# The middle of each FP4 quantisation on GpSimd instead of VectorE

## The chip, the cores and the metric

The kernel runs on one core of one Trainium2 chip. The metric is device time in microseconds (us), the median of several runs; smaller is better. Engines are named as the profile names them: PE is TensorE (matmuls and transposes), PEld its weight loads, ACT is ScalarE, DVE is VectorE, POOL is GpSimd, and SP is the queue that issues all DMAs here.

## What is computed

The input `x` has 8 batches of 1024 tokens with 512 features, in float32. One block is computed from the layer-normalised tokens, with two branches that are added to `x`:

```python
xn = _layernorm(x)
x = x + attn(xn, W_attn, b_attn, W_proj, b_proj) + ffn(xn, w_gate, w_up, w_down)
```

`attn` is causal attention with 16 heads of 32 features. `ffn` is a gated network with 1408 hidden features, in which the inputs and the weights of each of its three products are first quantised to FP4 and back:

```python
def fp4_quant_dequant(x):               # blocks of 16 along the last dimension
    scale = max(abs(block)) / 6.0       # one per block, at least 1e-12
    xn = block / scale
    idx = searchsorted(_MID, abs(xn))   # to the nearest of 0 .5 1 1.5 2 3 4 6
    return _GRID[idx] * sign(xn) * scale
def fp4_linear(x, w):
    return einsum(fp4_quant_dequant(x), fp4_quant_dequant(w))
h = silu(fp4_linear(x, w_gate)) * fp4_linear(x, w_up)
return fp4_linear(h, w_down)
```

The change is about the engine that does parts of `fp4_quant_dequant`.

## The kernel before

**Tiles.** Tokens go in tiles of 128 (64 in all), two tiles making a "twin" of 256 tokens. `prepare` (L387) normalises a twin, transposes it on PE (`transposed`, L324), and computes queries, keys and values (`project`, L435), which go to DRAM and come back by units of two heads (64 units). `scored` (L547) computes a unit's scores (L603), their row minima on DVE (L616, L619) and the exponentials on ACT (L575, into `part`). `weigh` (L666) transposes these on PE (L708), copies the result from PSUM on ACT (L711, into `pr`; a memset on POOL at L716 clears the corner), and multiplies with the values (L686). `network` (L749) does the FFN of a twin in six jobs of 512 columns (the sixth of 256): the products with `wgT` and `wuT` (L803), silu on ACT (L815) and the product with it on DVE (L820), giving `hid`; then `down` multiplies the quantised `hid` with `wdT` (L765). `finish` (L880) projects the attention's result (L895, L896, L904, L909) and stores the sum. All of it shares five PSUM banks (`Banks`, L180).

**Quantisation.** An instance of `Quantised` (L258) is a piece of at most 128x512 that is quantised in place. There are three kinds: 34 pieces of the weights (`weights_quantised`, L334; 28 of them while the first 16 tiles are prepared, six later), two halves of `xqT` for each of the 32 twins (`quantised`, L415), and the six `hid` of a twin (`hidden`, L819). Its steps, all on DVE before the change: for `xqT` and `hid` a transpose in 32x32 blocks (L263); the maximum of each block of 16 (L300); three small operations on the scales (L303 to L305); the product with the inverse scale (L317); the exponent of every element by a bit mask (L309) and a limit and factor on it (L312), which together give `step`; `step` added and subtracted (L319, L320), which rounds; the product with the scale (L321); and the transpose back.

**The order of the work** is written out when the kernel is built, by a plan with a clock in it: each engine has a time `free[...]`, each instruction adds a cost that the code states, and `merge` (L983) takes steps from several streams (attention's two halves, the network, the preparation, `finish`) so that PE has work whose inputs the plan believes ready. Every engine then executes its own queue in that written order, waiting on semaphores. The steps of pieces to be quantised lie in the list `background`; `passed` (L161) issues the next step of the first piece whenever the plan's DVE is about to be idle:

```python
idle = max(clock[0], free["dve"] - FILL, background[0].after)
```

A stream that needs a piece waits until the plan's `ready()` (L275), an estimate from the costs still left on DVE. The plan is not told how two engines affect one another.

**What POOL does before the change:** a power for each tile's normalisation (L378, 128x1), the memset at L716, and the bias added to a tile of the residual (L781, 128x512).

## Time and profile before

| | |
|---|---|
| median of 3 runs | 4223.45 us (4218.54 to 4223.89) |
| the profiled execution | 4220.1 us |
| its span, first to last instruction | 4218.2 us |
| mean granted PE clock | 0.994 of full speed |
| busy in the span | PE 4064.8, DVE 3061.9, ACT 2170.3, POOL 145.1 us |
| read from and written to HBM | 399.51 and 168.30 MB, 135 GB/s over the span |

The profile is one execution. A line of it names an engine, a line of the kernel (L321), an operation, and the tile written and those read (`hid<-hid,scale`). "PE bank L328 <- DVE hid L321" means that PE's instruction of line 328 waited, with PE idle, for DVE's instruction of line 321. A PE that is busy is not necessarily at its peak, since the ends of matmuls are modelled. The span falls into three parts: up to about 400 us the weights are quantised and the first tiles prepared; then attention, network and preparation run together, in a pattern that repeats every 127.3 us (a twin) until about 3200 us, when all tiles are prepared, and without preparation until about 4100 us; in the rest the last twin's network and the last eight tiles are finished.

### The profile page before, as it was taken

The numbers are of one execution on the slowest core, as the hardware profiler recorded it, in microseconds if no ns is written. First come the engines' busy times: TensorE is split into PE (matmuls) and PEld (weight loads), VectorE is DVE, ScalarE is ACT, GpSimd is POOL, SyncE is SP. The second block draws the span as 40 slices with busy tenths as digits, with TensorE's granted clock in tenths as the row PEclk, the third lists the DMA queues.
The fourth block names the chain that finished last, engine by engine and source line by source line (L and its number), as shares of the span: only waits on it lengthen the run. The fifth ranks groups of instructions, "written<-read, shape, count | busy, mean of one in ns | idle before, by whom it ended". The sixth has DMA issues, their size and how long they took to land.

```text
span 4218.2 us, 66169 instructions
## 1 busy us (share of the span) xinstructions
PE 4064.8 (96%) x22868; PEld 3008.8 (71%) x22868; DVE 3061.9 (73%) x7128; ACT 2170.3 (51%) x5342; POOL 145.1 (3%) x202
## 2 busy tenths in 40 slices
PE   8889999999999999999999999999999999999997
PEld 7766777777777777777777777777777666666665
DVE  7886776776766687766777766777666777777775
ACT  2245555555555555555555555555555555555540
POOL 0000000000000000000000000000000000000000
PEclk9999999999999999999999999999999999999999
DMA  6654443455555555555555555555554433333314
GB/s 194 197 162 120 123 118 113 130 143 148 160 143 152 147 142 153 165 140 146 155 143 149 160 142 150 150 143 152 157 144 116 116 91 95 95 94 96 96 57 129
DMA packets 550894, 572.21 MB, mean 136 GB/s; under 512 B 112416, under 2 KB 415520, under 8 KB 550560
## 3 DMA queue, kind: packets, MB, share of 16 engines
q1 hardware_dynamic: 550560, 567.99, 48.3%
q8 instruction: 181, 2.97, 0.3%
q14 instruction: 153, 1.25, 0.1%
HBM read 399.51 MB, written 168.30 MB: 135 GB/s over the span
## 4 chain that ended last, share of the span: by engine, by line
PE 87%; ACT 4%; DVE 3%; DMA 1%; issue 1%; SPq 0%; ACTq 0%; DVEq 0%
PE bank L803 29%; PE acc L765 14%; PE bank L708 11%; PE bank L448 9%; PE bank L603 8%; PE y L686 7%; PE bank L904 5%; PE bank L493 4%; ACT pr L711 2%; ACT part L575 1%; DVE bank L619 1%; PE bank L328 0%; DMA qs<-inv_kept 0%; DMA out_dram<-qs 0%; ACT full L504 0%
## 5 line engine op out<-in xcount | busy, mean ns | idle before, releaser
L711 ACT COPY pr<-bank 128x512 f32<-128x512 f32 (+1 forms) x1280 | 665.3, 548 | 811.2 <-PE bank L708 761.1
L575 ACT ACTIVATE part<-bank,neg 128x512 f32<-128x512 f32 (+3 forms) x1536 | 881.3, 583 | 183.5 <-DVE neg L619 151.3
L603 PE MATMUL bank<-ks,qs 128*128 128x512 f32 (+3 forms) x1536 | 715.8, 486 | 28.0 <-ACT pr L711 14.6
L708 PE MATMUL bank<-ident,part 128*128 128x128 f32 x4608 | 672.4, 274 | 32.2 <-ACT pr L711 17.2
L803 PE MATMUL bank<-xqT,wgT 128*128 128x256 f32 x2816 | 674.5, 384 | 19.4 <-ACT pr L711 17.4
L803 PE MATMUL bank<-xqT,wuT 128*128 128x256 f32 x2816 | 667.8, 381 | 0.0
L708 PEld LDWEIGHTS bank<-ident,part 128*128 128x128 f32 x4608 | 548.4, 141 | 160.5 <-ACT part L575 34.3
L765 PE MATMUL acc<-wdT,hid 128*128 128x512 f32 x1408 | 655.0, 595 | 3.1 <-DVE hid L263 3.1
L803 PEld LDWEIGHTS bank<-xqT,wgT 128*128 128x128 f32 x2816 | 516.5, 190 | 120.9 <-ACT pr L711 26.7
L803 PEld LDWEIGHTS bank<-xqT,wuT 128*128 128x128 f32 x2816 | 515.8, 190 | 68.1 <-issue 7.4
L616 DVE TENSOR_REDUCE neg<-bank 128x1 f32<-128x512 f32 x512 | 350.5, 685 | 292.1 <-PE bank L603 287.6
L603 PEld LDWEIGHTS bank<-ks,qs 128*128 128x128 f32 x1536 | 281.2, 189 | 248.1 <-issue 144.2
L619 DVE CUSTOM_DVE_ANT_0 bank<-bank,mask,neg 128x128 f32<-128x128 f32 (+3 forms) x512 | 284.5, 556 | 155.0 <-PE bank L603 123.6
L765 PEld LDWEIGHTS acc<-wdT,hid 128*128 128x128 f32 x1408 | 247.9, 190 | 208.2 <-issue 200.7
L686 PE MATMUL y<-pr,vs 128*32 128x256 f32 (+1 forms) x5120 | 356.0, 371 | 0.0
L448 PE MATMUL bank<-xnT,wa 128*128 128x256 f32 x1536 | 351.6, 382 | 0.2 <-ACT part L575 0.2
L448 PEld LDWEIGHTS bank<-xnT,wa 128*128 128x128 f32 x1536 | 287.4, 191 | 47.7 <-issue 10.8
L575 ACT ACTIVATION_READ_ACCUMULATOR part<-bank,neg 128x1 f32 x1536 | 314.2, 205 | 0.0
L619 DVE CUSTOM_DVE_ANT_0 bank<-bank,mask 128x128 f32<-128x128 f32 (+3 forms) x512 | 251.8, 496 | 84.4 <-PE bank L603 56.2
L460 ACT ACTIVATE full<-bank,bqk 128x256 f32<-128x256 f32 x256 | 107.3, 470 | 396.6 <-PE bank L448 335.5
L820 DVE TENSOR_TENSOR hid<-hid,bank 128x512 f32<-128x512 f32 x192 | 123.3, 642 | 253.4 <-PE bank L803 252.5
L263 DVE STREAM_TRANSPOSE hid<-hid 128x512 f32<-128x512 f32 (+1 forms) x384 | 245.9, 653 | 5.4
(79 smaller groups left out, 4115.9 us busy)
## 6 DMA issues: line engine op xcount, KB each, us to landing
wa<-in_L_attn_W_attn_dram SPq DMA_DIRECT2D x146, 512.0 KB, 3.7
qs<-qk_kept SPq DMA_DIRECT2D x512, 128.0 KB, 4.2
ks<-qk_kept SPq DMA_DIRECT2D x512, 128.0 KB, 4.1
wp<-in_L_attn_W_proj_dram SPq DMA_DIRECT2D x81, 512.0 KB, 3.8
qk_kept<-high SPq DMA_DIRECT2D x128, 256.0 KB, 3.0
qk_kept<-full SPq DMA_DIRECT2D x128, 256.0 KB, 3.0
y_kept<-yu SPq DMA_DIRECT2D x256, 128.0 KB, 2.4
yT<-y_kept SPq DMA_DIRECT2D x112, 256.0 KB, 3.5
```

What stands on the lines that cost most here:

```text
L263: turn = [(0.69, 0.0, lambda: nc.vector.transpose(out=xs, in_=xs))] if turned else []
L448: nc.tensor.matmul(pq[:, j, :], lhsT=halves[j][:, c, :], rhs=xnT[:, c, :], start=(c == 0), stop=(c == NC - 1),)
L575: nc.scalar.activation(parts[part][:, j * n : (j + 1) * n], banks.tiles[bank][:, j * n : (j + 1) * n], AF.Exp, bias=least, scale=1.0 if h ...
L603: nc.tensor.matmul(sc[:, j * n : (j + 1) * n], lhsT=un.qs[Q][:, r, i * P : (i + 1) * P], rhs=un.ks[h][:, r, :n], start=True, stop=True,)
L616: nc.vector.tensor_reduce(neg[:, 1, k : k + 1], one, AX.X, ALU.max, negate=True)
L619: nc.vector.tensor_tensor_reduce(one, one, mask[:, W - n :], scale=-1.0, scalar=neg[:, 1, k : k + 1] if Q else 3e38, op0=ALU.add, op1=ALU.min,
L686: nc.tensor.matmul(y[row : row + HD, base + q0 : base + QW], lhsT=un.vs[h][:, jj, r * HD : (r + 1) * HD], rhs=pr[:, r, q0:], start=(j < 2) ...
L708: nc.tensor.transpose(turned[:, r, i * P : (i + 1) * P], parts[part][:, at : at + P], ident)
L711: nc.scalar.copy(pr[:, :, i0 * P :], turned[:, :, i0 * P :])
L765: nc.tensor.matmul(twin.accs[i], lhsT=hqT[:, j, i * P : (i + 1) * P], rhs=wdT[:, n, :], start=(n == 0), stop=(n == NI - 1),)
L803: nc.tensor.matmul(job.g[:, j * QW : (j + 1) * QW], lhsT=wT[:, c, n * P : (n + 1) * P], rhs=job.twin.xqT[:, c, :], start=(c == 0), stop=(c ...
L904: nc.tensor.matmul(po, lhsT=yT[:, c, :], rhs=wp[:, c, :], start=(c == 0), stop=(c == NC - 1))
```

## The change

A piece can be `helped`: then the product with the inverse scale, the limit and factor (L312 before), the addition, the subtraction and the product with the scale are issued on POOL; the maximum, the scales, the exponents and the transposes stay on DVE. Pieces of `xqT` and `hid` are always helped; a piece of the weights is when the plan's POOL, with what is queued on it and 8.0 us more, would be through before the plan's DVE with 4.85 us more. In the order that results, 11 of the 34 weight pieces are. `passed` now takes the piece whose next step can start first, over both engines, and each step waits in the plan for the end of the piece's step before it and 0.2 us (`HOP`). `ready()` counts the load of both. The buffers of the scales grow from four to six, and `step` has one buffer for each engine in place of two.

```diff
--- before.py
+++ after.py
@@ -82,6 +82,8 @@
     LATE = 0.6
     SURE = 0.4
     FILL = 0.4
+    HELPED = 8.0
+    ALONE = 4.85
     HOP = 0.2
     TABLE = 1.3
     AHEAD_OF_OTHERS = 0.6
@@ -95,6 +97,7 @@
     p2 = ctx.enter_context(tc.tile_pool(name="p2", bufs=2))
     p3 = ctx.enter_context(tc.tile_pool(name="p3", bufs=3))
     p4 = ctx.enter_context(tc.tile_pool(name="p4", bufs=4))
+    p6 = ctx.enter_context(tc.tile_pool(name="p6", bufs=6))
     p8 = ctx.enter_context(tc.tile_pool(name="p8", bufs=8))
     dram = ctx.enter_context(tc.tile_pool(name="dram", bufs=6, space=DRAM))
     ps_g = ctx.enter_context(tc.tile_pool(name="ps_g", bufs=1, space=PSUM))
@@ -158,14 +161,20 @@
 
     background = []
 
+    def next_in_background():
+
+        first = {}
+        for one in background:
+            first.setdefault(one.left[0][0], one)
+        times = ((max(clock[0], free[e] - FILL, one.end - FILL, one.after - HOP), one) for e, one in first.items())
+        return min(times, key=lambda entry: entry[0], default=(float("inf"), None))
+
     def passed(us):
         end = clock[0] + us
         while True:
             first = min(waiting_list, key=lambda e: e.due, default=None)
             due = first.due if first is not None else float("inf")
-            idle = float("inf")
-            if background:
-                idle = max(clock[0], free["dve"] - FILL, background[0].after)
+            idle, one = next_in_background()
             if min(due, idle) > end:
                 break
             if due <= idle:
@@ -174,7 +183,7 @@
                 first.now()
             else:
                 clock[0] = idle
-                background[0].one()
+                one.one()
         clock[0] = end
 
     class Banks:
@@ -258,17 +267,23 @@
     class Quantised:
 
 
-        def __init__(self, src, w, xs, after=0.0, turned=False):
+        def __init__(self, src, w, xs, after=0.0, turned=False, helped=None):
             self.out, self.after, self.end = xs, after, 0.0
-            turn = [(0.69, 0.0, lambda: nc.vector.transpose(out=xs, in_=xs))] if turned else []
-            steps = turn + self.operations(src, w, xs) + turn
-            self.left = [(us + wide * w / CW, action) for wide, us, action in steps]
+            if helped is None:
+                helped = self.queue("pool") + HELPED < self.queue("dve") + ALONE
+            turn = [("dve", 0.69, 0.0, lambda: nc.vector.transpose(out=xs, in_=xs))] if turned else []
+            steps = turn + self.operations(src, w, xs, helped) + turn
+            self.left = [(engine, us + wide * w / CW, action) for engine, wide, us, action in steps]
             background.append(self)
 
+        def queue(self, engine):
+            behind = sum(us for one in background for e, us, _ in one.left if e == engine)
+            return max(clock[0], free[engine]) + behind
+
         def one(self):
-            us, action = self.left.pop(0)
+            engine, us, action = self.left.pop(0)
             action()
-            self.end = dve(us, self.after - HOP)
+            self.end = on(engine, us, max(self.end, self.after - HOP))
             if not self.left:
                 background.remove(self)
 
@@ -276,7 +291,9 @@
             if not self.left:
                 return self.end
             ahead = background[: background.index(self) + 1]
-            return max(clock[0], self.after) + 1.3 * sum(us for one in ahead for us, _ in one.left)
+            load = {e: sum(us for one in ahead for f, us, _ in one.left if f == e) for e in ("dve", "pool")}
+            own = sum(us for _, us, _ in self.left)
+            return max(clock[0], self.after) + max(own, 1.3 * load["dve"], load["pool"])
 
         def wait(self):
 
@@ -288,15 +305,16 @@
                 self.one()
             return self.out
 
-        def operations(self, src, w, xs):
+        def operations(self, src, w, xs, helped):
             nb = w // BLOCK
             blocks = lambda a: a.rearrange("p (n e) -> p n e", e=BLOCK)
             spread = lambda a: a.unsqueeze(2).broadcast_to([P, nb, BLOCK])
             scale, inv, step = [], [], []
+            name, eng, two, one = ("pool", nc.gpsimd, 1.28, 0.75) if helped else ("dve", nc.vector, 0.7, 0.43)
 
             def maximum():
-                scale.append(p4.tile([P, CW // BLOCK], F32, name="scale")[:, :nb])
-                inv.append(p4.tile([P, CW // BLOCK], F32, name="inv")[:, :nb])
+                scale.append(p6.tile([P, CW // BLOCK], F32, name="scale")[:, :nb])
+                inv.append(p6.tile([P, CW // BLOCK], F32, name="inv")[:, :nb])
                 nc.vector.tensor_reduce(scale[0], blocks(src), AX.X, ALU.max, apply_absolute_value=True)
 
             def scales():
@@ -304,21 +322,22 @@
                 nc.vector.reciprocal(inv[0], scale[0])
                 nc.vector.tensor_scalar_mul(inv[0], inv[0], 1.0 - 2.0**-24)
 
+            def exponents():
+                step.append(p2.tile([P, CW], F32, name=f"step_{name}", bufs=1)[:, :w])
+                nc.vector.tensor_scalar(step[0].bitcast(I32), xs.bitcast(I32), 0x7F800000, None, ALU.bitwise_and)
+
             def powers():
-                step.append(p2.tile([P, CW], F32, name="step")[:, :w])
-                nc.vector.tensor_scalar(
-                    step[0].bitcast(I32), xs.bitcast(I32), 0x7F800000, None, ALU.bitwise_and
-                )
-                nc.vector.tensor_scalar(step[0], step[0], 1.0, 1.5 * 2.0**22, ALU.max, ALU.mult)
+                eng.tensor_scalar(step[0], step[0], 1.0, 1.5 * 2.0**22, ALU.max, ALU.mult)
 
             return [
-                (0.68, 0.0, maximum),
-                (0.2, 0.5, scales),
-                (0.7, 0.0, lambda: nc.vector.tensor_tensor(blocks(xs), blocks(src), spread(inv[0]), ALU.mult)),
-                (0.87, 0.0, powers),
-                (0.7, 0.0, lambda: nc.vector.tensor_tensor(xs, xs, step[0], ALU.add)),
-                (0.7, 0.0, lambda: nc.vector.tensor_tensor(xs, xs, step[0], ALU.subtract)),
-                (0.7, 0.0, lambda: nc.vector.tensor_tensor(blocks(xs), blocks(xs), spread(scale[0]), ALU.mult)),
+                ("dve", 0.68, 0.0, maximum),
+                ("dve", 0.2, 0.5, scales),
+                (name, two, 0.0, lambda: eng.tensor_tensor(blocks(xs), blocks(src), spread(inv[0]), ALU.mult)),
+                ("dve", 0.43, 0.0, exponents),
+                (name, one, 0.0, powers),
+                (name, two, 0.0, lambda: eng.tensor_tensor(xs, xs, step[0], ALU.add)),
+                (name, two, 0.0, lambda: eng.tensor_tensor(xs, xs, step[0], ALU.subtract)),
+                (name, two, 0.0, lambda: eng.tensor_tensor(blocks(xs), blocks(xs), spread(scale[0]), ALU.mult)),
             ]
 
     def transposed(dst, src, n):
@@ -421,7 +440,7 @@
         nc.sync.dma_start(out=xqT, in_=twin.xnT)
         yield 0.0, clock[0] + 5.0, 0, 0.1
         halves = [xqT[:, c : c + NC // 2, :].rearrange("p c t -> p (c t)") for c in (0, NC // 2)]
-        working = [Quantised(half, NC // 2 * QW, half, clock[0], turned=True) for half in halves]
+        working = [Quantised(half, NC // 2 * QW, half, clock[0], turned=True, helped=True) for half in halves]
         for one in working:
             yield from one.wait()
             one.done()
@@ -820,7 +839,7 @@
             nc.vector.tensor_tensor(job.hid, job.hid, job.g, ALU.mult)
             end = dve(0.7, max(job.gated, clock[0] + 1.72))
             banks.back(job.bank, end)
-            job.hq = Quantised(job.hid, job.w, job.hid, end, turned=True)
+            job.hq = Quantised(job.hid, job.w, job.hid, end, turned=True, helped=True)
 
         def jobs():
             for twin in twins:
```

## The prediction

> **What bounds the kernel now.** I read the page first: busy shares, then the chain of waits. Columns of the first line: busy us (share of the span) x instructions.
>
> ```profile
> PE 4064.8 (96%) x22868; PEld 3008.8 (71%) x22868; DVE 3061.9 (73%) x7128; ACT 2170.3 (51%) x5342; POOL 145.1 (3%) x202
> ...
> PE 87%; ACT 4%; DVE 3%; DMA 1%; issue 1%; SPq 0%; ACTq 0%; DVEq 0%
> ```
>
> TensorE (PE) is the bound: 87% of the chain that ended last is PE. VectorE (DVE), which the change relieves, holds 3% of it. So no sum of DVE time saved is a gain; only PE's idle time is on offer. The table by stage says where that lies (stage, length, busy us of PE, PEld, DVE, ACT, POOL, granted PE clock, DMA):
>
> ```profile
> 0.00:400.00 400.00, 339.16 (x1774) 270.93 (x1774) 307.87 (x705) 156.93 (x385) 17.12 (x36) 0.94 0.59 172
> 400.00:4100.00 3700.00, 3632.11 (x20739) 2669.61 (x20738) 2688.94 (x6302) 2010.51 (x4953) 125.02 (x164) 1.00 0.48 132
> 4100.00:4218.00 118.00, 93.57 (x360) 68.23 (x358) 65.05 (x122) 2.88 (x6) 2.94 (x2) 0.99 0.41 118
> ```
>
> PE is idle 61 us in the first 400, 68 in the next 3700, 24 in the last 118. The waits of PE, first for the stage 0 to 400, then 400 to 4100 (us in total, times, longest):
>
> ```profile
> PE bank L328 <- DVE hid L321: 22.3, 9, 4.7
> PE bank L328 <- DVE xt L382: 15.6, 1, 15.6
> ```
> ```profile
> PE bank L803 <- ACT pr L711: 17.4, 38, 0.8
> PE bank L708 <- ACT pr L711: 15.3, 30, 0.8
> PE bank L603 <- ACT pr L711: 13.6, 35, 0.5
> PE bank L708 <- ACT part L575: 7.4, 28, 0.6
> ```
>
> At the start PE waits 22.3 us for quantised weights from DVE (the 15.6 are the first normalisation, which the change leaves alone). In the middle it waits for ScalarE (ACT) to empty PSUM banks, less than 1 us at a time; DVE stands behind only a part of that.
>
> **What the change takes off DVE.** The order of instructions shows which pieces move: all 64 halves of `xqT`, all 192 of the network's `hid` (160 of 512 columns, 32 of 256), and 11 of the 34 weight pieces; 23 stay on DVE. Per full piece DVE loses four two-input operations (rows of L317, L319, L320, L321: 0.69 each) and L312 (0.43): 4 x 0.69 + 0.43 = 3.19 us; per half piece 4 x 0.42 + 0.30 = 2.0. The steady state repeats every 127.3 us (two token tiles, a "period" from here; 32 in all) with 7 full pieces and a half: 7 x 3.19 + 2.0 = 24.3 us of the 90.6 us that DVE is busy in it. All in all 32 x 24.3 + 11 x 3.2 = 812 us.
>
> **What it puts on GpSimd (POOL).** A two-input 128x512 operation has a row: L781, 1.27 us. Not in the trace is the one-input limit-and-factor on POOL: from 0.43 (the same on DVE) to 1.27; I take 0.65, twice POOL's 128x256 memset (0.316), its nearest row by work. A piece: 4 x 1.27 + 0.65 = 5.7 us of POOL; a half piece between 2.9 and 5.7, taken as 3.0. A period: 7 x 5.7 + 3.0 = 43, and with the old 4.5 POOL is 37% busy. It does not become the bound (at 1.27 for the unknown operation 41%). `rstd` (L378), the memset (L716) and the residual (L781) now queue behind 1.27 us operations, at worst one each; the plan gives POOL a clock of its own and waits 0.2 us after every step, so I cost this at nothing beyond the stalls below. No DMA is issued by a moved step.
>
> A piece also crosses engines: DVE, POOL, DVE (exponents), POOL, DVE (transpose). Those two DVE instructions wait for POOL in DVE's queue, with the attention's L616 and L619 behind them.
>
> **The price: the two engines exclude one another.** At 4136 us the trace shows both at once (start, us, engine, line):
>
> ```profile
> 4135.52 0.69 DVE L319 TENSOR_TENSOR hid<-hid,step 128x512 f32<-128x512 f32 x1
> ...
> 4136.20 2.94 POOL L781 TENSOR_TENSOR res<-res,bp 128x512 f32<-128x512 f32 x2 [66.17 <-DMA res<-in_L_attn_x_dram]
> 4136.25 1.77 DVE L320 TENSOR_TENSOR hid<-hid,step 128x512 f32<-128x512 f32 x1
> 4138.05 1.64 DVE L321 TENSOR_TENSOR hid<-hid,scale 128x512 f32<-128x512 f32 x1
> ```
>
> DVE's 0.69 became 1.77 and 1.64: waits of 1.08 and 0.95; POOL's pair, 2.50 elsewhere, took 2.94. They alternate: DVE ends at 4138.02 and 4139.69, so one operation of each takes 1.67 us, where DVE alone needs 2 x 0.72. One-input TENSOR_SCALARs are held too (L305 at 3316.16: 0.78 in place of 0.18); beside the same POOL rows, transposes (0.71), reductions and L619 on PSUM (0.63) run at their usual lengths.
>
> The Trainium skill speaks against the change here: "SBUF — State Buffer", section "Who interferes with whom", has GpSimd and a VectorE instruction of two SBUF inputs or of a two-port mode block each other for the whole instruction. The rows above agree in kind; for the whole 1.27 the pair of operations would take 0.69 + 1.27 = 1.96, the trace has 1.67.
>
> **Stage 0 to 400, taken as -12 us.** In its saturated stretches a weight piece takes DVE 5.31 us (reductions at 114.52, 119.83 and 125.14), 3.98 of it operations that POOL excludes (4 x 0.69, 2 x 0.43, 2 x 0.18). With POOL beside it, two pieces need 3.98 + 0.79 (the helped piece's own on DVE) + 4 x 0.98 + some 0.5 = 9.2 us, against 10.6: 13% better, not 50%. So I take a third of the 22.3 us of waiting, 7, and 5 for the clock: it is 0.91 between 100 and 300, and 0.77 between 120 and 150, just after the waits for DVE at 115 to 125. Bounds: nothing gained and 15 lost if POOL pieces come later than the plan holds (it doesn't know of the exclusion), to all 22 and 8 of clock.
>
> **Stage 400 to 4100, taken as -16 + 6 us.** Relief: the waits behind DVE's results (all of ACT part L575, 12.3 in this stage, and DVE part L909, 2.3) halve, -7; of the 46.3 us for L711 I take a fifth, -9, since a bank with scores is held until DVE has reduced it. Bounds: 0 to -60 of the 68. Stalls: 30 DVE instructions of a period can be held (L303 and L305 8 each, L473 and L474 4 each, L382 2, L895 and L896 2 each), 37% of the time, for half of 1.08: 6 us a period, so DVE's net relief is 24.3 - 6. What of it reaches PE the trace measures in four places: at 3316 DVE lost 0.60 + 1.01 us, and 8 us later PE waited 0.53 for DVE part L909; at 3744, 0.80 + 1.01 and 0.74. Both leave 1.07 us of slack. One stall is absorbed, two in a row pass on half a microsecond. The second piece of a pair meets this (4 pieces a period); if 10% of them pass on 0.5, 32 x 4 x 0.05 = 6. Bound: all pass, +64.
>
> **Stage 4100 to 4218, taken as +3.** Only the last two pieces bear on the end. From L317 to the transpose the last full one took 4.0 us (4154.03 to 4158.06), on POOL 4 x 1.27 + 0.65 + 0.43 = 6.2 and hops: +2.5, the half piece behind it +0.5. PE already waited for both (2.37 and 0.75), so it is paid in full. 0 to +6.
>
> **Sum.** -12 - 16 + 6 + 3 = -19 from the profiled execution's span of 4218.2 gives 4199. That execution took 4220.1, the median is 4223.45; the same offset gives **4204**.
>
> **Rivals.**
> (1) *The stalls reach PE: slower.* Place: scales (L303, L305) and casts on DVE beside POOL's four-operation runs, with L616 and L619 behind. For it: PE has 2% idle in the middle and a written order, so a late bank isn't made up for. Against: the measured slack of 1.07. The gains are 12 + 16 - 3 = 25, so it decides from 25 / 32 = 0.8 us passed on a period. At 1.7 a period, with the start's gain gone: 54 - 16 + 3 = +41, 4264; its middle case (1.2 and the start unchanged) 38 - 16 + 3 = +25, 4248.
> (2) *Nothing comes of it.* PE's 3632 busy us stay, one set of 0.5 us gaps takes another's place; the prologue is held by the exclusion, with 23 of 34 weight pieces on DVE as before. 4223.
> (3) *DVE was behind most bank waits.* All of 22 and 8 at the start, half of 68 in the middle, tail +3: -61, 4162. For it: DVE stays below 60% afterwards; against: ACT's own 51% and its table loads.
>
> **Chances.** A measurement here can tell about 0.2% (8.4 us) from no change. Forecast 0.40, (3) 0.15, (2) 0.15, (1) 0.30. Faster: 0.55, same 0.15, slower 0.30. Range: from 4155 (just past (3)) to 4255 (past (1)'s middle case; the rest is left out).
>
> **What would show it.** Right: POOL near 1580 us busy, DVE near 2470, POOL's two-input steps (L335, L338 to L340 of the changed kernel) at 1.3 with some at 1.7, DVE casts and scales with a second length about 1 us longer; PE's waits for hid L321 down to about 15; PE's idle time in 400 to 4100 near 58. Wrong: that idle time at 90 or above (rival 1), a POOL one-input operation above 1.3, or new waits of PE for POOL (the memset). What would upset the sum most is a period unlike 127.3 us, 0.3 us of it being 10 us in all.

## The result, and the profile after

| | before | after |
|---|---|---|
| median | 4222.88 us (6 runs, 4216.81 to 4223.89) | 4253.92 us (6 runs, 4248.41 to 4256.69) |
| span of the profiled execution | 4218.2 us | 4250.4 us |
| ratio of the times | | 1.0075, 95% interval 1.0063 to 1.0088 |

The change makes the kernel slower by 0.75%. The forecast was 4204 us, faster; the time lies inside the range and between the two cases of rival (1), 4248 and 4264.

The page of the changed kernel, busy shares and the chain by engine:

```profile
PE 4074.1 (96%) x22868; PEld 3011.5 (71%) x22868; DVE 2408.8 (57%) x5793; ACT 2167.8 (51%) x5342; POOL 1826.2 (43%) x1537
...
PE 79%; ACT 4%; DVE 4%; POOL 3%; DMA 2%; issue 1%; SPq 1%; DVEq 0%; ACTq 0%; POOLq 0%
```

The work moved as described: DVE lost 653 us of busy time. In the chain PE fell from 87% to 79%, and POOL, which was not in it, has 3%. POOL got 1681, where the forecast had 1435 (1580 less 145). The same columns by stage as before:

```profile
0.00:400.00 400.00, 332.03 (x1736) 266.05 (x1736) 291.55 (x621) 152.39 (x374) 120.04 (x110) 0.94 0.57 169
400.00:4100.00 3700.00, 3617.21 (x20617) 2654.27 (x20614) 2058.56 (x5056) 2002.20 (x4943) 1656.16 (x1385) 1.00 0.48 132
```

PE is idle 68 us of the first 400 (61 before) and 83 of the next 3700 (68 before). The excess of POOL's time has one line. Its operations on a full piece, in the groups by form (busy us, mean ns of one | idle before):

```profile
L330 POOL TENSOR_SCALAR step_pool<-step_pool 128x512 f32<-128x512 f32 x234 | 451.5, 1930 | 322.0 <-DVE step_pool L327 319.8 <-DVE row_sums L666 2.2
L339 POOL TENSOR_TENSOR hid<-hid,step_pool 128x512 f32<-128x512 f32 x170 | 224.8, 1322 | 13.2
L338 POOL TENSOR_TENSOR hid<-hid,step_pool 128x512 f32<-128x512 f32 x170 | 218.5, 1285 | 14.2
L335 POOL TENSOR_TENSOR hid<-hid,inv 128x512 f32<-128x512 f32 x170 | 184.3, 1084 | 896.4 <-DVE inv L323 799.9 <-DVE row_sums L666 68.4 <-issue 11.4
L340 POOL TENSOR_TENSOR hid<-hid,scale 128x512 f32<-128x512 f32 x170 | 182.5, 1073 | 13.3
```

Limit-and-factor (L330), with one input, takes 1.93 us: longer than the operations with two. The forecast took 0.65 and bounded it by 1.27; the changed kernel's plan holds 0.75. A piece is 1.08 + 1.93 + 1.29 + 1.32 + 1.07 = 6.7 us of POOL and not 5.7. DVE's waits for POOL, which the forecast costed at nothing (us in total, times, longest):

```profile
DVE hid L274 <- POOL hid L340: 208.4, 126, 5.9
DVE xqT L274 <- POOL xqT L340: 71.7, 31, 3.1
...
DVE step_pool L327 <- POOL hid L335: 47.2, 51, 1.2
...
DVE step_pool L327 <- POOL xqT L335: 13.4, 29, 1.2
```

PE's waits in the stage 400 to 4100 (columns alike):

```profile
PE bank L622 <- ACT pr L730: 27.5, 64, 0.8
PE bank L727 <- ACT part L594: 21.2, 56, 1.3
PE bank L622 <- ACT part L594: 16.9, 27, 0.8
PE bank L822 <- ACT pr L730: 8.8, 25, 0.5
```

L622, L727, L822, L594 and L730 are the lines 603, 708, 803, 575 and 711 of before. In this stage PE waits for POOL nowhere. The waits for `part` (L594), which the forecast halved, went up. At the start, 0 to 400, PE does wait for POOL, in a line that is new:

```profile
PE bank L347 <- DVE hid L340: 21.4, 10, 4.7
...
PE bank L347 <- POOL hid L340: 13.1, 7, 7.8
```

L347 transposes the quantised weights on PE (L328 before), and L340 is the last operation of a piece on either engine. Together PE waits 34.5 us for weights, where it waited 22.3 for DVE alone before and the forecast expected about 15.

**Where the 32 us lie.** The transposes of the row statistics (PE L653 before, L672 after) come once in each of the 64 units, so their starts mark the same work in both traces. In the changed kernel unit 8 is 8.2 us late (756.6 for 748.4), unit 48 30.2 (3311.7 for 3281.5), unit 63 25.2 (4109.8 for 4084.6), the end 32.2. So the start costs **+8.2**, the steady state **+22.0**, the phase after it **-5.0**, the end **+7.0**. In the steady state the period went from 127.3 to 128.5 us.

**One place in each period.** The timeline of the changed kernel where the period of 1346 to 1475 us loses its time (start, us, engine, line; other lines left out):

```profile
1421.51 1.06 POOL L340 TENSOR_TENSOR hid<-hid,scale 128x512 f32<-128x512 f32 x1
1421.58 1.27 DVE L492 CAST high<-full 128x512 fp32r<-128x512 f32 x1 [2.71 <-DMA inv_y<-inv_kept]
...
1422.52 1.24 POOL L335 TENSOR_TENSOR hid<-hid,inv 128x512 f32<-128x512 f32 x1
...
1422.88 1.43 DVE L493 TENSOR_TENSOR full<-full,high 128x512 fp32r<-128x512 f32 x1
...
1424.23 0.48 DVE L638 CUSTOM_DVE_ANT_0 bank<-bank,mask,neg 128x256 f32<-128x256 f32 x1
...
1424.81 0.69 ACT L594 ACTIVATE part<-bank,neg 128x512 f32<-128x512 f32 x1 [2.14 <-DVE neg L638]
...
1425.64 0.38 PE L622 MATMUL bank<-ks,qs 128*128 128x256 f32 x1 [0.82 <-ACT part L594]
```

L492 and L493 split the rows of queries and keys (L473, L474 before). Beside no POOL instruction the cast takes 0.43 and the subtraction 0.69. Here the cast starts beside the last operation of one piece on POOL, the subtraction beside the first of the next, and both are held: 1.27 + 1.43 for 0.43 + 0.69, 1.58 us more. The maximum of the scores (L638) stands behind them in DVE's queue, the exponentials (L594) wait for it, PE waits 0.82 us for these. This gap, of 0.82 us each time, comes 18 times in all, 128.5 us apart; the casts ahead of it start at 907.6, 1036.1, 1164.6 and so on. Another held pair in nearly every period (the cast 0.81, the subtraction 1.64, at 1381.0 for instance) has no gap above 0.3 us ahead of PE's L622 in the 6 us behind it.

### The profile page after: what moved, and what is told of

The parts are those of the page before. It is cut to its first block, busy times and chain, and to the rows that moved or that the text cites. A ratio compares the mean times of both kernels' runs of the same rounds, so it can differ in the third digit from the quotient of the medians.

```text
span 4250.4 us, 66406 instructions
## 1 busy us (share of the span) xinstructions
PE 4074.1 (96%) x22868; PEld 3011.5 (71%) x22868; DVE 2408.8 (57%) x5793; ACT 2167.8 (51%) x5342; POOL 1826.2 (43%) x1537
## 3 DMA queue, kind: packets, MB, share of 16 engines
q14 instruction: 156, 1.28, 0.1%
## 4 chain that ended last, share of the span: by engine, by line
PE 79%; ACT 4%; DVE 4%; POOL 3%; DMA 2%; issue 1%; SPq 1%; DVEq 0%; ACTq 0%; POOLq 0%
PE bank L822 27%; PE acc L784 13%; PE bank L727 10%; PE bank L467 7%; PE y L705 6%; PE bank L622 6%; PE bank L923 5%; PE bank L512 4%; ACT pr L730 2%; ACT part L594 2%; DVE bank L638 1%; POOL step_pool L330 1%; DVE full L493 1%; DVE high L492 1%; POOL hid L339 1%
## 5 line engine op out<-in xcount | busy, mean ns | idle before, releaser
L730 ACT COPY pr<-bank 128x512 f32<-128x512 f32 (+1 forms) x1280 | 664.0, 548 | 721.4 <-PE bank L727 667.5
L594 ACT ACTIVATE part<-bank,neg 128x512 f32<-128x512 f32 (+3 forms) x1536 | 882.3, 585 | 279.4 <-DVE neg L638 270.1
L622 PE MATMUL bank<-ks,qs 128*128 128x512 f32 (+3 forms) x1536 | 703.0, 480 | 51.7 <-ACT pr L730 28.3
L727 PE MATMUL bank<-ident,part 128*128 128x128 f32 x4608 | 672.9, 275 | 27.1 <-ACT part L594 23.5
L822 PE MATMUL bank<-xqT,wgT 128*128 128x256 f32 x2816 | 677.5, 385 | 11.7 <-ACT pr L730 8.8
L822 PE MATMUL bank<-xqT,wuT 128*128 128x256 f32 x2816 | 670.0, 381 | 0.8
L727 PEld LDWEIGHTS bank<-ident,part 128*128 128x128 f32 x4608 | 543.1, 140 | 174.0 <-issue 55.6
L330 POOL TENSOR_SCALAR step_pool<-step_pool 128x512 f32<-128x512 f32 (+2 forms) x267 | 487.2, 1825 | 346.0 <-DVE step_pool L327 343.8
L822 PEld LDWEIGHTS bank<-xqT,wgT 128*128 128x128 f32 x2816 | 514.9, 190 | 118.6 <-issue 26.2
L335 POOL TENSOR_TENSOR hid<-hid,inv 128x512 f32<-128x512 f32 (+1 forms) x203 | 205.1, 1010 | 898.5 <-DVE inv L323 799.9
L822 PEld LDWEIGHTS bank<-xqT,wuT 128*128 128x128 f32 x2816 | 518.0, 190 | 67.6 <-ACT part L594 3.0
L622 PEld LDWEIGHTS bank<-ks,qs 128*128 128x128 f32 x1536 | 280.6, 189 | 260.5 <-issue 137.6
L638 DVE CUSTOM_DVE_ANT_0 bank<-bank,mask,neg 128x128 f32<-128x128 f32 (+3 forms) x512 | 283.3, 553 | 220.5 <-PE bank L622 192.0
L638 DVE CUSTOM_DVE_ANT_0 bank<-bank,mask 128x128 f32<-128x128 f32 (+3 forms) x512 | 251.5, 498 | 160.3 <-PE bank L622 142.0
L397 POOL TENSOR_TENSOR rstd<-rstd,power 128x1 f32<-128x1 f32 x64 | 45.8, 716 | 651.3 <-DVE rstd L396 651.3
```

What stands on the lines that cost most here:

```text
L330: eng.tensor_scalar(step[0], step[0], 1.0, 1.5 * 2.0**22, ALU.max, ALU.mult)
L594: nc.scalar.activation(parts[part][:, j * n : (j + 1) * n], banks.tiles[bank][:, j * n : (j + 1) * n], AF.Exp, bias=least, scale=1.0 if h ...
L622: nc.tensor.matmul(sc[:, j * n : (j + 1) * n], lhsT=un.qs[Q][:, r, i * P : (i + 1) * P], rhs=un.ks[h][:, r, :n], start=True, stop=True,)
L638: nc.vector.tensor_tensor_reduce(one, one, mask[:, W - n :], scale=-1.0, scalar=neg[:, 1, k : k + 1] if Q else 3e38, op0=ALU.add, op1=ALU.min,
L727: nc.tensor.transpose(turned[:, r, i * P : (i + 1) * P], parts[part][:, at : at + P], ident)
L730: nc.scalar.copy(pr[:, :, i0 * P :], turned[:, :, i0 * P :])
```

## The experiments

I went in with the theory of a **late piece** (DVE waits in its queue for a POOL that takes 1.93 us where the plan holds 0.75) and its rivals **port** (operations held while the other engine reads or writes SBUF) and **new order** (the rewritten planner writes a worse order, wherever the work runs). The table sums up all runs; each is timed against the kernel before on the same chip. fills, hop_true_fills, fill_products and fill_limit leave out part of the quantisation; all the others compute everything. "Steps" are the differences from before in the four parts of the span as above: start, steady state, the phase after it, end. They come from one execution each: psum and psum_tail, whose written order is the same up to the end, differ by 2.4 us at the start, so a step is good to 2 or 3 us.

| kernel | us | ratio to before, 95% interval | steps, us |
|---|---|---|---|
| after | 4253.9 | 1.0063 to 1.0088 | +8.2 +22.0 -5.0 +7.0 |
| weights_only | 4273.7 | 1.0105 to 1.0135 | +8.6 +28.0 +10.6 +5.9 |
| main_only | 4265.6 | 1.0085 to 1.0115 | +20.3 +22.4 -5.2 +5.3 |
| none_helped | 4272.8 | 1.0103 to 1.0134 | +11.8 +27.1 +10.9 +5.3 |
| plan_true | 4269.7 | 1.0090 to 1.0124 | +15.8 +7.7 +15.0 +12.1 |
| hop | 4294.0 | 1.0157 to 1.0188 | +13.6 +51.8 +4.1 +5.1 |
| n_hop | 4218.2 | 0.9984 to 1.0003 | +0.5 -11.2 +6.9 +3.1 |
| hop_true | 4263.4 | 1.0086 to 1.0117 | +12.8 +29.5 -7.6 +6.8 |
| fills | 4216.0 | 0.9980 to 0.9999 | -2.8 +2.2 -5.2 +5.5 |
| hop_true_fills | 4213.9 | 0.9970 to 0.9990 | -1.0 +2.5 -13.6 +7.5 |
| hop_true_psum | 4224.7 | 0.9999 to 1.0018 | +6.0 +3.8 -7.7 +4.2 |
| n_hop_psum | 4242.3 | 1.0033 to 1.0063 | -2.6 +20.8 +8.7 -0.7 |
| psum | 4215.2 | 0.9976 to 0.9995 | -3.3 -1.3 -5.1 +5.0 |
| before_nudged | 4231.5 | 1.0013 to 1.0032 | -6.0 +2.2 +15.3 -0.4 |
| after_nudged | 4260.3 | 1.0076 to 1.0106 | +23.5 +22.4 -5.8 +5.6 |
| psum_tail | 4212.1 | 0.9966 to 0.9984 | -5.7 -0.9 -5.0 +2.1 |
| psum_limit | 4233.7 | 1.0019 to 1.0037 | +4.1 +7.7 +2.8 -2.0 |
| fill_products | 4208.7 | 0.9964 to 0.9983 | -6.3 -1.9 -5.6 +3.1 |
| fill_limit | 4213.2 | 0.9974 to 0.9993 | -6.1 -3.0 -5.0 +4.1 |

### How much is only the order: before_nudged and after_nudged

```diff
-                ("dve", 0.68, 0.0, maximum),
+                ("dve", 0.72, 0.0, maximum),
```

> The kernel before with one price of its plan moved by 0.04 us (the maximum of a quantisation, 0.68 to 0.72), the work untouched; over a thousand of TensorE's 8385 rows stand elsewhere in the written order. If the order of before is one of many equal ones: 4222 us within 6. If any new order costs (the 51 us of the kernel without helped pieces would then be a re-roll and not the 0.2 us charge): 4235 or more.

> The changed kernel with the same 0.04 us on the same price. If the loss is the change's and not the order's: 4254 us within 8. If the written order decides: anywhere from 4215 to 4275, and the 31 us of loss says little of the change.

Any edit of a price has the plan write another order. That alone moved before by +9 and after by +6 us. So between kernels of different order a difference of some 10 us is read as nothing here. The steps say more than the sums: the nudge moved the start of the changed kernel from +8.2 to +23.5 and the last phase of before by +15.3, but the steady state stood, +22.0 and +22.4 in the changed kernel, 0 and +2.2 in before. The +22 is the change's; the +8 of the start is no more than the order alone can do.

### Which pieces, and the planner alone: weights_only, main_only, none_helped

```diff
-    working = [Quantised(half, ..., turned=True, helped=True) for half in halves]
+    working = [Quantised(half, ..., turned=True, helped=False) for half in halves]   # weights_only, none_helped
-    job.hq = Quantised(job.hid, job.w, job.hid, end, turned=True, helped=True)
+    job.hq = Quantised(job.hid, job.w, job.hid, end, turned=True, helped=False)      # weights_only, none_helped
-    done.append((piece, Quantised(raw, piece[4], raw)))
+    done.append((piece, Quantised(raw, piece[4], raw, helped=False)))                # main_only, none_helped
```

> The pieces of xqT and hid stay on VectorE; of the weights' pieces, those that the rule chooses may still go to GpSimd. Late piece (VectorE waits in its queue for a GpSimd operation that takes 1.93 us where the plan holds 0.75) and port (VectorE's operations held beside GpSimd's) both put the prologue's share here alone: unit 8 began 8.2 us later in the changed kernel, so about 4232 us (4226 to 4238), and the period back at 127.3. New order (the rewritten planner alone costs the time, wherever the work runs): the period stays at 128.5, about 4250.

> The weights' pieces stay on VectorE; those of xqT and hid go to GpSimd as in the changed kernel. Late piece and port: the prologue's +8 goes, the period of 128.5 (18 periods at +1.2) and the tail's +7 to +11 stay: about 4245 us (4238 to 4252). If the changed kernel's loss came mainly from the prologue's shift: under 4232. New order: 4250 again.

> No piece goes to GpSimd, but the rewritten planner, the split of exponents from limit-and-factor, and the deeper buffers stay. Late piece and port: the time of before, 4223 us (4217 to 4230), period 127.3. New order: 4245 or more, period near 128.5.

A miss for both of the theories that I held: with nothing on POOL the rewritten planner gives 4273, 50 us above before and 19 above the changed kernel. Leaving pieces out does not separate the parts of the change, because the rewritten planner then charges its own price, of which the next section tells, to more steps on DVE. What main_only does show is that the steady +22.4 stands without any weight piece on POOL.

### What in the planner: n_hop, hop, hop_true, plan_true

`self.end = on(engine, us, max(self.end, ...))` adds the 0.2 us of a hop behind every step, also where the next is on the same engine. A piece on DVE alone is planned some 1.6 us too long.

```diff
-            self.end = on(engine, us, max(self.end, self.after - HOP))
+            start = self.end if engine != self.last else self.end - HOP
+            self.last = engine
+            self.end = on(engine, us, max(start, self.after - HOP))     # hop, n_hop (with no piece helped), hop_true
-            name, eng, two, one = ("pool", nc.gpsimd, 1.28, 0.75) if helped else ...
+            name, eng, two, one = ("pool", nc.gpsimd, 1.28, 1.95) if helped else ...     # hop_true, plan_true
```

> Only the plan's price of limit-and-factor on GpSimd is changed, from 0.75 to 1.95 us, so that VectorE's operations behind a piece are written later; the work and its engines are those of the changed kernel. Late piece: VectorE's waits for GpSimd (126 of 5.9 us' sum 208 for the transposes of hid, 51 for the exponents) shrink to under a third, and most of the steady +22 us goes: 4228 to 4238 us. Port: the operations lie beside each other as before, 4248 to 4258 us. If the time goes up beyond 4258, the later writing of the pieces itself delays the down products.

> The changed kernel, with the plan's 0.2 us between two steps of a piece charged only where the engine changes; the changed planner charges it behind every step, so that a piece on VectorE alone is planned about 1.6 us longer than before the change, and one on GpSimd 5 steps longer by 1.0. Late plan (this charge is what costs the time; the work on GpSimd itself gains, as 4254 against 4273 without any piece there says): 4204 us (4195 to 4225). Late piece (VectorE waits in its queue for GpSimd's 1.93 us operation): the plan for GpSimd gets shorter still, 5.9 us for a measured 6.6, VectorE's waits grow, 4254 to 4275 us.

> No piece on GpSimd, and the 0.2 us charged only where the engine changes; what is left of the rewritten planner is that exponents and limit-and-factor are two steps of VectorE and not one. Late plan: back to 4223 us (4216 to 4232) from 4273. Any new order costs (the written order of before was a lucky one): about 4250 to 4275 again.

> As the kernel with the 0.2 us only where the engine changes, and the plan's price of limit-and-factor on GpSimd at 1.95 us. Late plan with late piece as a second, smaller cost: VectorE's waits for GpSimd shrink and the time is at or below that kernel's, 4198 to 4212 us. Late piece alone: this one falls by 15 us or more below the kernel with the short price. Port: no difference between the two beyond 4 us.

With the charge gone and nothing on POOL the time is 4218, no different from before: the charge, not any new order, costs 55 us in a kernel that quantises on DVE. But for helped pieces it seems to be a mistake that helped: 4 x 1.28 + 0.75 + 5 x 0.2 = 6.87 us planned for the 6.7 that POOL takes. Without it the plan holds 6.27 (two of the five steps on POOL follow one on DVE and keep their 0.2), and the kernel, hop, is at 4294. In it DVE waits 322 us (208) for the last operation on `hid`, and of PE's waits over the whole span this line (L727 and L594 of the changed kernel) grew most, from 23.5 in the changed kernel:

```profile
PE bank L729 <- ACT part L596: 52.4, 58, 2.7
```

With L330 at its measured price as well (hop_true) the kernel comes back to 4263, 31 us better: a plan that thinks POOL faster than it is does cost. But a fair plan with helped pieces is 45 us behind the same plan without. plan_true has the right price and the charge, a piece at 8.07 us: the steady state gets most of its loss back (+7.7), but the last phase and the end lose 27 against before. These four kernels differ in their order throughout, so what their plans do is argued here, and not shown place by place.

### The port, in an unchanged order: fills, hop_true_fills

```diff
+            def fill(tile, *widths):
+                for wide in widths:
+                    nc.gpsimd.memset(tile[:, : max(1, wide * w // CW)], 0.5)
+    # helped pieces: L335 2 x 512 (and one column of inv); L330 3 x 512 and 256; L338, L339 2 x 512 and 128; L340 2 x 512 columns
```

> The order and the plan of the changed kernel; each of GpSimd's five operations of a piece is a set of MEMSETs of about its length (2 of 512 columns for 1.07 us, 3 and one of 256 for 1.93, 2 and one of 128 for 1.28), which read nothing. It leaves out the middle of the helped quantisations. Port: VectorE's 135 us of holding go, and what of it reaches TensorE: 4235 us or less. Late piece or late plan: no change beyond 5 us, 4249 to 4259 us, with VectorE's waits for GpSimd as before.

> The kernel with the fair plan (0.2 us only where the engine changes, limit-and-factor on GpSimd at 1.95 us), with GpSimd's five operations of a piece replaced by MEMSETs of about the same length, as in the fills kernel; it leaves out the middle of the helped quantisations. With no piece on GpSimd this planner gave 4218, with GpSimd's real operations 4263. Port: the 45 us go again, 4222 us or less (4205 to 4228). Late piece (VectorE's waits in its queue for GpSimd, which stay): 4255 to 4268 us.

These issue the changed kernel's (hop_true's) instructions on PE and DVE in the same order; POOL only writes, for about the same time. They gave back 38 us (4254 to 4216) and 50 (4263 to 4214). The order is kept, and with it the plan's charge, and the steady state is at +2.2: neither is what costs the changed kernel there. DVE's waits in its queue for POOL stayed: 410 us in fills, 341 in the changed kernel. So these waits by themselves cost PE nothing, as the forecast had it, and late piece as I had put it falls. Holding didn't vanish: in 45 of the 58 times that the cast lay beside a MEMSET of a piece it was held, to 0.72 us in the mean. The subtraction of two SBUF tiles took 0.69 in all 56 such times. Over all its instances, first in the changed kernel, then in fills:

```profile
L493 DVE TENSOR_TENSOR full<-full,high 128x512 fp32r<-128x512 f32 x128 | 131.7, 1029 | 4.4
```
```profile
L512 DVE TENSOR_TENSOR full<-full,high 128x512 fp32r<-128x512 f32 x128 | 88.6, 692 | 4.4
```

### Which operations of POOL: fill_products, fill_limit

```diff
-                if helped:                      # fills
+                if helped and k != 1:           # fill_products: L330 real, the other four MEMSETs
-                    widths = ((512, 512), (512, 512, 512, 256), ...)[k]
+                if helped and k == 1:           # fill_limit: only L330, one MEMSET of 0.53 us
+                    nc.gpsimd.memset(step[0], 0.5)
```

> The changed kernel with its order; of GpSimd's five operations of a piece the four with two inputs are replaced by MEMSETs of about the same length, and limit-and-factor stays real at 1.93 us. It leaves out the products, sum and difference of the helped pieces. Port through the two-input operations (they held the subtraction of the q and k rows to 1.43 and 1.64 us from 0.69, which limit-and-factor and MEMSETs did not): most of the 38 us go, 4214 to 4228 us. Late piece: 4248 or more, since GpSimd's piece is as long as before.

> The changed kernel with its order; only limit-and-factor on GpSimd is replaced, by one MEMSET of 0.53 us, which leaves out that step of the helped pieces. GpSimd's piece falls from 6.6 to 5.2 us. Late piece: VectorE's waits for GpSimd fall to under half and the time by 10 us or more, 4244 or less. Port: the two-input operations stay, so the time stays at 4245 to 4258 us; what it falls by is the price of having taken 0.65 for 1.93.

Both in the order of the changed kernel, and each alone takes the whole loss away: 45 us without the two-input operations, 41 with L330 at 0.53 us. They are not two costs to be added but the two conditions of one. The same place in fill_limit, where POOL's lines 346 and 340, DVE's 508, 509 and 654, ACT's 610 and PE's 638 are the changed kernel's L340, L335, L492, L493, L638, L594 and L622:

```profile
1399.61 1.06 POOL L346 TENSOR_TENSOR hid<-hid,scale 128x512 f32<-128x512 f32 x1
...
1400.63 1.06 POOL L340 TENSOR_TENSOR hid<-hid,inv 128x512 f32<-128x512 f32 x1
...
1401.12 0.85 DVE L508 CAST high<-full 128x512 fp32r<-128x512 f32 x1 [1.55 <-ACT full L495]
...
1402.01 0.69 DVE L509 TENSOR_TENSOR full<-full,high 128x512 fp32r<-128x512 f32 x1
...
1403.19 0.69 ACT L610 ACTIVATE part<-bank,neg 128x512 f32<-128x512 f32 x1 [0.98 <-DVE neg L654]
...
1404.12 0.36 PE L638 MATMUL bank<-ks,qs 128*128 128x256 f32 x1
```

With L330 shorter by 1.40 us, POOL's last operation on the piece starts 1.51 us ahead of the cast and not 0.07. The cast then is held once, by 0.42, the subtraction not at all, and PE has no gap. PE's order is the same, so the two can be compared instruction by instruction. The changed kernel loses 1.07 us to fill_limit at this one matmul, and between -0.24 and +0.21 at the three other places of that period where they differ by over 0.12: 1.22 at the four. With all smaller differences the period is 1.37 us longer. The same matmul loses 1.06 or 1.07 in each of the 18 periods, 19.2 in all, of the 25.1 us that separate the two steady states; against fills it is 19.2 of 19.9.

How much is held in all is no measure: the scale operation L323 is held more in fill_limit (0.49 us in the mean of all its instances) than in the changed kernel (0.27). Where a hold falls decides.

### The two victims out of the port's way: psum, hop_true_psum, n_hop_psum

```diff
-                        full[:, j, :],
+                        pq[:, j, :],                      # ACT writes the biased rows back into the bank
...
-                    nc.vector.tensor_copy(high, full)
-                    nc.vector.tensor_tensor(low, full, high.bitcast(F32), ALU.subtract)
+                    nc.vector.tensor_copy(high, pq)
+                    nc.vector.tensor_tensor(low, pq, high.bitcast(F32), ALU.subtract)
+                    banks.back(k, ready)                  # and not behind ACT
```

> The fair plan, GpSimd's real operations, and VectorE's cast and subtraction of the q and k rows reading PSUM in place of SBUF (ScalarE writes its biased rows back into the bank, the bank is freed behind VectorE). Of VectorE's operations in the changed kernel's trace those that read PSUM were not held beside GpSimd. Port through these two operations (66 of some 112 us of holding): the holding goes, and most of the 45 us with it: 4225 to 4240 us. Port through the small scale operations, or late piece: no change, 4258 to 4270 us.

> The control: the same two operations read PSUM, with no piece on GpSimd and the fair plan (4218 us without this edit). All theories: 4218 us within 8; if it is off by more, the later freeing of the bank has a price of its own, by which the kernel with GpSimd's pieces is to be corrected.

> The changed kernel itself (its own plan, 4254 us) with VectorE's cast and subtraction of the q and k rows reading PSUM. Port through these two: 4225 to 4238 us, of the 38 us that the fills gave back. Port through the scale operations or late piece: 4248 to 4260 us.

The plan also charges DVE 1.4 us for the two in place of 1.15. With PSUM as their input, cast and subtraction are not held any more, in groups by form of psum:

```profile
L492 DVE TENSOR_TENSOR full<-bank,high 128x512 fp32r<-128x512 f32 x128 | 88.5, 691 | 4.4
L491 DVE CAST high<-bank 128x512 fp32r<-128x512 f32 x128 | 88.3, 690 | 183.9 <-ACT bank L479 183.4
```

and the time falls by 39 us in either plan, to 4215 and 4225, the steady +22.0 to -1.3. The order is another than the changed kernel's, so this is weaker evidence than the fills; but the control went the other way. Without pieces on POOL the same edit costs 24 us (n_hop_psum, 4242 for 4218), against the expectation. Whether that comes from the bank's later return or from the order, which changes too, was not tried.

### The end, and limit-and-factor on DVE: psum_tail, psum_limit

```diff
-    job.hq = Quantised(..., turned=True, helped=True)
+    job.hq = Quantised(..., turned=True, helped=job.twin is not twins[-1] or job.first < NI - 3)     # psum_tail
-                eng.tensor_scalar(step[0], step[0], 1.0, 1.5 * 2.0**22, ALU.max, ALU.mult)
+                nc.vector.tensor_scalar(step[0], step[0], 1.0, 1.5 * 2.0**22, ALU.max, ALU.mult)     # psum_limit
```

> The kernel with the cast and subtraction from PSUM (4215 us), with the last two pieces of hid of the last pair of tiles on VectorE and not on GpSimd; TensorE's order is the same row by row. Late piece at the end (TensorE waited 7.9 us once for the last transpose of hid, which waited for GpSimd): the tail's 10 us fall to 2, 4206 to 4209 us. Port or order: no change.

> The kernel with the cast and subtraction from PSUM (4215 us), with limit-and-factor of helped pieces on VectorE (0.43 us by its own rows) in place of GpSimd's 1.93; the plan's price goes with it. Late piece: GpSimd's piece falls from 6.6 to 4.7 us, VectorE's waits for it to under half, and the time by 4 to 10 us: 4205 to 4211. Port: nothing, 4211 to 4219, or up by what one more round trip between the engines and the new order cost.

With the last two pieces on DVE the end takes 2.9 us less (+2.1 for +5.0), PE's one wait for the last transpose 3.9 us for 7.9. The expected 8 were too many. Psum_tail, at 4212.1, is the fastest kernel here that computes everything: 0.25% faster than before (interval of the ratio 0.9966 to 0.9984), 1% faster than the change as made. Psum_limit is 18 us slower than psum; its order differs throughout, its loss is spread over the start, steady state and last phase, and its cause stays open.

## Why the prediction was wrong

**The price of L330 failed.** The forecast had it "from 0.43 (the same on DVE) to 1.27; I take 0.65"; it measured 1.93, beyond the upper bound. That bound assumed that one input can't cost more than two on the same engine, which no row showed. The sum used this price only for the end, but it also set where POOL stood when the casts came. Fill_limit, with 0.53 in place of 1.93, is the run nearest to the forecast's assumption, though its MEMSET reads nothing: 4213 us, 9 from the forecast, on its side of before. Its terms are -6.1 for the forecast's -12, -8.0 for -10 and +4.1 for +3.

**The stalls, "32 x 4 x 0.05 = 6", were the term that turned the sum, and failed by their kind.** Exclusion, its victims and the chain by L619 (now L638) to PE were named rightly, also that two holds in a row are what passes. But I made a rate of it, 10% of many. The order is written and repeats, so there is one place that meets both holds in 18 periods: 18 x 1.07 = 19 us at the one matmul, of the 22.0 that the steady state lost against before and of the 25.1 against fill_limit. The other held pair in nearly every period is free. The slack of 1.07, read from two single events, is not the slack here: of 1.58 held 1.07 were lost, so it is some 0.5; at the pair that leaves no gap (0.38 + 0.95 held) it is over 1.3.

**The relief, -16 over 400 to 4100, was twice what there is.** Without the collision, in the same order, steady state and last phase give -3.0 and -5.0 (fill_limit), -1.9 and -5.6 (fill_products). Halving what waits for `part` had no ground in the rows; in this order the steady state has nearly no time that DVE's speed decides.

**The start, -12, came out as +8.2.** Of the 12, 7 were to come from PE's waits for weights and 5 from the clock. The waits went up, from 22.3 to 34.5 us, 13.1 of them for POOL, and the granted clock of the first 400 us is 0.94 before and after. The three kernels in the changed kernel's order that replace POOL's operations are 11.0 to 14.5 us earlier than it at unit 8, at -2.8 to -6.3 against before. So a quarter to a half of the gain exists, and 11 us go away in fills, whose pieces are as long on POOL as here: they are a price of the real operations, not of the order or of a piece's length alone. Which instructions pass it on was not traced. Only the bound "15 lost if POOL pieces come later than the plan holds" took in the real one. The order has luck of the same size: the nudge alone gave another +15.

**The end, +3, was +7.0,** +3.1 to +5.5 in the fills. A piece on POOL is 1.3 longer by L330 than forecast; psum_tail finds 2.9 us of the end in the two pieces on POOL. The rest was not tried.

**The waits in DVE's queue for POOL, put at nothing, held** for the waits in themselves (fills). The plan's times for POOL must be near the real ones, though: hop, where they are shorter, is 40 us slower. That the plan's charge of 0.2 us "after every step" also lies between steps on one engine I had read and passed over: it costs a DVE-only kernel 55 us, and here it made up for most of what the wrong 0.75 left out.

**Rival (1) was right** in sign, size (4248 to 4264 for 4254) and place, "casts on DVE beside POOL's four-operation runs, with L616 and L619 behind"; it was to decide from 0.8 us a period, and 1.2 passed. It got 0.30. That its middle case, 4248, comes so near is partly luck: its 38 - 16 + 3, with no change at the start, stands for +22.0, -5.0, +8.2 and +7.0. Of its victims the casts and the subtractions behind them passed their holds on; no gap of PE was traced to the scales.

Of the signs of being wrong that the prediction named, two appeared: a one-input operation on POOL above 1.3 us (1.93), and new waits of PE for POOL (13.1 us at the start, for weights and not for the memset). PE's idle time in 400 to 4100 was 83 us, above the 58 forecast and below the 90 that was to decide for rival (1).

The Trainium skill, "SBUF — State Buffer", section "Who interferes with whom", says that a VectorE instruction with two SBUF inputs contends with a GpSimd one that reads SBUF, and not with one that only writes it. It also says that casts can enter a two-port mode, in which they contend with GpSimd, and that an instruction with at most one SBUF input and outside those modes does not. Most runs agree: the subtraction took 1.43 us beside a product and 0.69 beside MEMSETs, the cast 0.72 beside MEMSETs, and both took 0.69 with an input from PSUM. One differs: beside limit-and-factor alone, which also reads SBUF, the subtraction kept its 0.69 in all 19 cases in hop and in 19 of 22 in hop_true, though 3 of the 4 in plan_true were held, to 0.98. Its "GPSIMD Engine Reference", section "4.1 Engine selection", calls one-input operations on GpSimd "roughly line-rate" and those of two inputs about twice slower than VectorE's. Here the first took 1.93 us for VectorE's 0.43, the second 1.07 to 1.32 for 0.69. The measurement decides: the one-input operation was the worst one to move.

## What to carry to other kernels

When a written order repeats, don't price contention as a share of many events: lay the two engines' rows over one period, ask which few instructions in front of the bound engine meet it, and multiply by the number of periods. An operation that no trace shows on an engine may cost more there than one with more inputs; price it by a run, or bound it without that assumption. And before blaming a moved operation, run the rewritten planner with nothing moved, and a nudged price for the size of luck.

## What the runs showed of the hardware

- POOL's time by columns, from the 512- and 256-column rows of the changed kernel: limit-and-factor (one input, two operations) 1.93 and 1.07 us, so 3.4 ns a column; sum and difference 1.29 and 0.73, 2.2 ns; the products with a scale for each block 1.08 and 0.62, 1.8 ns.
- A MEMSET on POOL, which reads no tile, also holds DVE's cast (from 0.43 to a mean of 0.72 us, in 45 of 58 cases in fills) and the small scale operation L321 (from 0.18 to a mean of 0.39, in 123 of 151), but in none of 56 cases the subtraction of two SBUF tiles.
- Beside POOL, in the changed kernel, the transposes of `hid` (0.71 us, 188 cases beside it), the block maxima (0.68, 102 cases) and what DVE reads from PSUM (L638 on 128x512 0.75, 58 cases) kept their times; in psum so did the cast and the subtraction from PSUM (0.69 us, 128 times each). The cast itself is slower from PSUM, 0.69 for 0.43.
